# Picking one row of a group on VectorE instead of lowering the others in TensorE's sum

## The chip, the cores and the metric

One core of a Trainium2 chip runs the kernel; the other cores are idle. The metric is device time in microseconds, the median of three runs. Beside the timed runs there is one profiled execution, and all views below are of that one.

## The reference

The kernel computes one message-passing layer of a graph network. `x` has 12500 nodes of 32 features, `src` and `dst` name 400000 edges sorted by `dst`, and every edge has 32 attributes of its own.

```python
h = jnp.maximum(_layernorm(x, axis=-1), 0.0)
e_feat = jnp.concatenate([h[src], h[dst], edge_attr], axis=-1)   # 400000 x 96
v = jax.nn.relu(e_feat @ W1 + b1) @ W2 + b2                      # 96 -> 64 -> 32
x_cand = jax.ops.segment_max(v, dst, num_segments=12500)
out = x + jnp.maximum(x_cand, h)
```

Note that `h` is never negative, because of the relu after the normalisation.

## The kernel before

The edges are cut into four stripes (`NS`) that lie side by side on the partitions, 32 partitions each. A stripe is walked in 196 chunks of 512 edges (`NCH`, `C`), so a chunk holds 2048 edges. The main loop takes two chunks per turn (98 turns); `a` and `b` are the two chunks of the next turn, which are prepared while the current ones, `c` and `c+1`, are finished.

The rows `h[src]` of a chunk come to SBUF as 16 sets of 128 rows, in two ways:

- 12 sets are gathered from DRAM by indirect DMAs that GpSimd (POOL) issues, one per set (`gather`, L148: 2345 of them in all). They go into a ring of 24 buffers of three sets each, so POOL can run up to 72 sets ahead. Nothing else stands on POOL's queue during the loop.
- 4 sets (`MM`) are picked by TensorE from a copy of `h` that stays in SBUF (`hs`), split in a high and a low part of type fp32r. This is `tile(c, m)`, 780 times in all. The 12544 nodes are 128 partitions x 7 groups (`A1`) x 14 places (`A0`). `one_hots` builds, for each of the 7 groups, a 128x512 matrix `hot[:, k]` that has a one where the partition and the group are those of the edge's source: one VectorE tensor_scalar per group (L340) that compares the chunk's keys `kb` with a column of `key_p`. Fourteen matmuls (7 groups x 2 parts, L356) with moving operands of 448 columns sum up, in one PSUM bank `po`, all 14 nodes of the wanted group for each edge. To leave the right one of the 14, a fifteenth matmul (L353, bf16) comes first: `its`, a one-hot of the place (L342), times `others`, a constant with -1e30 at all other places. VectorE then takes the maximum over the 14 (L359), straight from PSUM.

`to_features` turns three gathered sets (L400) or the four picked ones (L403) into feature-major form `ht` by 32x32 transposes on VectorE. The rest of a turn: `into_ph` (L444) sums the three 64-wide products of an edge chunk in four PSUM banks `ph` (attributes by `edges_into`, the destination windows by `windows_into`, sources last); ScalarE applies the relu (`hid`, L491); the second product goes to two banks (L506); VectorE runs a maximum scan along the edges (L513); `leave_1` transposes the scan and adds the bias (`so`, L420, L422); `lasts` (L410) marks the last edge of each node; `leave_2` picks these rows (L430), ScalarE copies them (`wo`, L434), and SyncE (SP) writes them out. `window_hots` (L386, L387) builds the one-hots of the destination windows on ScalarE by a square and a relu. ScalarE's queue also issues the loads of `kb`, `db` and `pb`.

The order on PE, VectorE, ScalarE and SP is the order in which the code is written; no scheduler moves anything. The PSUM banks matter: `tile` and the second product share two buffers named `pv` in rotation. So a matmul group into `pv` waits until the group two before it has been read. [...]

A turn of the loop, in the order of writing (TensorE and VectorE parts):

```python
tile(a, 0); to_features(a, 0); into_ph(ht of c, c+1)      # then hid and window_hots on ScalarE
one_hots(b, range(3)); tile(a, 1); to_features(a, 1)
one_hots(b, range(3, A1)); lasts(c); tile(a, 2); to_features(a, 2)
edges_into(a); second product into pv, pv                 # L506
windows_into(a); leave(); scan, scan                      # L513
tile(a, 3); to_features(a, 3..J); leave_1(c); lasts(c + 1)
tile(b, 0); one_hots(a + 2, range(4)); leave_2(c); tile(b, 1); leave_1(c + 1)
one_hots(a + 2, range(4, A1)); tile(b, 2); tile(b, 3)     # each with its to_features
```

Ahead of the loop the layer normalisation, `hs`, the penalties and the checks are made, and the tiles of chunks 0 and 1 run by themselves.

Of the kernel before, what the change touches and what calls it, by code (L numbers as in the profile page):

```python
# [23 lines left out]
P = 128  # L24
N = 12500
E = 400000
D = 32
# [21 lines left out]
GP = 3  # L49
ROUND = 12582912.0  # L50
LOW = 1e30
ZERO = 784
WEIGHTS = 6 * HID + D + P + 1
EPS = 1e-5
# [2 lines left out]
def ap(t, offset, dims):  # L57
    return bass.AP(tensor=t.tensor, offset=t.offset + offset, ap=dims)
# [3 lines left out]
def gnn_kernel(ctx, tc, x, src, src_mm, src_t, dst, dst_next, dst_ext, lo, lo_c, hi, edge_attr, weights, w1, w2, b2, out):  # L62
# [26 lines left out]
    q_d = dram.tile([NP, HID], F32, name="q_d")  # L89
    pen_d = dram.tile([EP], BF16, name="pen_d")  # L90
    top_d = [dram.tile([NP, D], F32, name=f"top_d{k}") for k in range(2)]
    key_d = dram.tile([2, len(MMC) * MM * P], F16, name="key_d")
    acc_d = dram.tile([NP, D], F32, name="acc_d")
    v_d = dram.tile([P, D], F32, name="v_d")

# [21 lines left out]
    place = const.tile([P, 1], F32, name="place")  # L117
    nc.gpsimd.iota(place, pattern=[[0, 1]], base=0, channel_multiplier=1,
                   allow_small_or_imprecise_dtypes=True)
    key_p = const.tile([P, A1], F32, name="key_p")  # L120
    nc.gpsimd.iota(key_p, pattern=[[1, A1]], base=0, channel_multiplier=A1,
                   allow_small_or_imprecise_dtypes=True)
    hs = const.tile([P, 2, A1, D, A0], F32R, name="hs")
    others = const.tile([P, D, A0], BF16, name="others")


    wt = const.tile([P, WEIGHTS], F32, name="wt")
# [26 lines left out]
    with tc.tile_pool(name="nodes", bufs=1) as pool, tc.tile_pool(name="nodes_ps", bufs=2, space=PSUM) as ps:  # L154
# [10 lines left out]
        iota_a = pool.tile([P, D, A0], F32, name="iota_a")  # L165
        nc.gpsimd.iota(iota_a, pattern=[[0, D], [1, A0]], base=0, channel_multiplier=0,
                       allow_small_or_imprecise_dtypes=True)
# [15 lines left out]
        with tc.manual_schedule(engines={DVE, SP}):  # L183
# [35 lines left out]
            key16 = pool.tile([P, 2, len(MMC) * MM], F16, name="key16")  # L219
            nc.vector.tensor_copy(key16[:, 0], key)  # L220
            nc.vector.scalar_tensor_tensor(key16[:, 1], key, -float(A0), sp, op0=ALU.mult, op1=ALU.add)
            nc.sync.dma_start(key_d.rearrange("k (p e) -> p k e", p=P), key16)
# [84 lines left out]
    with tc.tile_pool(name="edges", bufs=3) as pool, tc.tile_pool(name="edges_ps", bufs=1, space=PSUM) as ps, \  # L307
# [3 lines left out]
        ofs = {}  # L311
        keys = {}
        hots = {}
        bases = {}
        iota_ps = ps.tile([P, C], F32, name="iota_ps")[:, :W]
        nc.vector.tensor_copy(iota_ps, iota_w)
        mm_rows = {}
        gh = {}
        hts = {}

        def load_keys(c):

            if c in MMC:
                n = min(2, MMC.stop - c)
                kb = pool.tile([P, 2, 2, MM * P], F16, name="kb", bufs=2)
                nc.scalar.dma_start(kb[:, :, :n], ap(key_d, (c - MMC.start) * MM * P,
                                                     [[0, P], [len(MMC) * MM * P, 2], [1, n * MM * P]]))
                for k in range(n):
                    keys[c + k] = kb[:, :, k]

        def one_hots(c, groups):

            if c not in MMC:
                return
            if c not in hots:
                hots[c] = (pool.tile([P, A1, MM * P], F32R, name="hot", bufs=2),
                           pool.tile([P, MM * P], BF16, name="its", bufs=2))
            hot, its = hots[c]
            for k in groups:
                nc.vector.tensor_scalar(hot[:, k], keys[c][:, 0], key_p[:, k:k + 1], None, op0=ALU.is_equal)  # L340
            if A1 - 1 in groups:
                nc.vector.tensor_scalar(its, keys.pop(c)[:, 1], place, None, op0=ALU.is_equal)  # L342

        def tile(c, m):

            if c not in MMC:
                return
            if m == 0:
                mm_rows[c] = pool.tile([P, MM, D], F32, name="gm", bufs=6)
            hot, its = hots[c]  # L350
            e = slice(m * P, (m + 1) * P)
            po = ps.tile([P, C], F32, name="pv", bufs=2)[:, :D * A0]
            nc.tensor.matmul(po, its[:, e], others.rearrange("p f a -> p (f a)"), start=True, stop=False)  # L353
            for k in range(A1):
                for part in range(2):
                    nc.tensor.matmul(po, hot[:, k, e], hs[:, part, k].rearrange("p f a -> p (f a)"),  # L356
                                     start=False, stop=(k == A1 - 1 and part == 1))
            rows = mm_rows[c][:, m, :]
            nc.vector.tensor_reduce(rows, po.rearrange("p (f a) -> p f a", a=A0), axis=AX.X, op=ALU.max)  # L359

        def load(c):
            if c % LOAD == 0:
# [26 lines left out]
        def to_features(c, part):  # L389

            if c >= NCH:
                return
            if c not in hts:
                hts[c] = pool.tile([P, K, D], F32, name="ht", bufs=4)
            ht = hts[c]
            n = min(K - MM * (c in MMC), (SE - c * C) // D)
            if part < J:
                r = slice(part * SOME, min((part + 1) * SOME, n))
                if r.start < n:
                    nc.vector.transpose(ht[:, r].rearrange("p k e -> p (k e)"),  # L400
                                        gh[c][part][:, :r.stop - r.start].rearrange("p k f -> p (k f)"))
# [74 lines left out]
        for c in range(0, NCH, 2):  # L476
# [33 lines left out]
            for x in range(2):  # L510
# [2 lines left out]
                nc.vector.tensor_tensor_scan(sm, loaded.pop(c + x)[2], pv[x], before, op0=ALU.add, op1=ALU.max)  # L513
# [178 lines left out]
```

## Time and profile before

| what | value |
|---|---|
| time, median of 3 runs | 3158.97 us (3158.54 to 3159.71) |
| profiled execution | 3161.57 us, its span 3159.8 us |
| granted TensorE clock | 0.983 |
| busy share of PE, DVE, ACT, POOL | 96%, 58%, 18%, 74% |
| matmuls of `tile` (L356, L353) | 10920 and 780 |
| gathers (L148) | 2345, the first at 31.1 us, the last at 3059.8 us |

A busy share is the union of the instructions' durations over the span. TensorE's instructions overlap each other, so what one of them costs is read from the distance between starts in the timeline, not from its duration. For VectorE and ScalarE the next instruction begins slightly before the last one's end when it doesn't depend on it. For POOL a gather has a duration and a constant pause behind it.

### The profile page before, as it was taken

What the parts mean: (1) busy time and instruction counts of PE and PEld (TensorE: products, weight loads), DVE (VectorE), ACT (ScalarE), POOL (GpSimd) and SP (SyncE); (2) the same over time, 40 slices, a digit from 0 to 9 for tenths busy, and PEclk for the clock granted to TensorE, in tenths of its full rate; (3) what the DMA queues carried; (4) which work ended last, traced back from release to release, by engine and by line L of the source; (5) the groups of instructions that cost most, each with busy time, mean ns of one, the idle gap of its engine ahead of it and who ended that gap; (6) DMA issues with size and microseconds to landing.
All of it is one profiled execution on the core that took longest, in us unless ns stands there. A gap on an engine that the chain in (4) does not pass through costs nothing. (4 is left out here: it accounts for less than half of the span.)

```text
span 3159.8 us, 59504 instructions
## 1 busy us (share of the span) xinstructions
PE 3038.9 (96%) x21969; PEld 2382.0 (75%) x21969; DVE 1822.4 (58%) x3999; ACT 562.8 (18%) x1007; POOL 2331.2 (74%) x2377
## 2 busy tenths in 40 slices
PE   2799999999999999999999999999999999999995
PEld 1578787777778777777778777777778777777873
DVE  6455555555555555555555555555555555555554
ACT  2121212112121212112121211112121211212121
POOL 7777777777777777777777777777777777777751
PEclk7899999999999999999999999999999999999997
DMA  6323332332333233233323332332333233233321
GB/s 246 109 64 74 90 73 63 90 80 68 72 89 76 64 84 83 71 69 89 78 64 77 88 72 63 90 83 64 73 89 76 64 87 85 66 72 88 78 57 63
DMA packets 203030, 255.38 MB, mean 81 GB/s; under 512 B 116062, under 2 KB 154862, under 8 KB 189551
## 3 DMA queue, kind: packets, MB, share of 16 engines
q10 hardware_dynamic: 42364, 138.10, 14.0%
q1 hardware_dynamic: 85330, 74.88, 10.1%
q0 software_dynamic: 75040, 38.57, 8.8%
q8 instruction: 173, 2.83, 0.4%
q14 instruction: 123, 1.00, 0.1%
HBM read 237.24 MB, written 14.05 MB: 80 GB/s over the span
## 5 line engine op out<-in xcount | busy, mean ns | idle before, releaser
L148 POOL DMA_INDIRECT gh<-h_d,src_i x2345 | 2301.2, 981 | 731.3 <-issue 567.8
L356 PE MATMUL pv<-hs,hot 128*128 128x448 f32 x10920 | 2435.0, 376 | 0.0
L356 PEld LDWEIGHTS pv<-hs,hot 128*128 128x128 f32 x10920 | 2058.5, 189 | 150.2 <-issue 0.3
L359 DVE TENSOR_REDUCE gm<-pv 128x32 f32<-128x448 f32 x780 | 486.3, 623 | 1149.9 <-PE pv L356 1147.7
L340 DVE TENSOR_SCALAR hot<-kb,key_p 128x512 fp32r<-128x512 f16 x1365 | 584.0, 487 | 6.1 <-DMA kb<-key_d 6.1
L491 ACT ACTIVATE hid<-ph,wt 128x512 f32<-128x512 f32 x392 | 237.2, 688 | 1325.7 <-PE ph L444 1312.2
L513 DVE TENSOR_TENSOR_SCAN sm<-pb,sm,pv 128x512 f32<-128x512 bf16 x195 | 249.6, 1280 | 133.4 <-PE pv L506 122.8
L353 PE MATMUL pv<-others,its 128*128 128x448 bf16 x780 | 281.3, 361 | 17.3 <-DMA qw<-q_d 10.6
L434 ACT ACTIVATE wo<-tr 128x64 f32<-128x64 f32 x196 | 43.7, 223 | 1146.6 <-PE tr L430 1056.4
L400 DVE STREAM_TRANSPOSE ht<-gh 128x96 f32<-128x96 f32 x782 | 209.5, 268 | 0.0
L353 PEld LDWEIGHTS <-its 128*128 128x128 bf16 x780 | 74.9, 96 | 172.4 <-issue 151.8
L430 PEld LDWEIGHTS tr<-so,last 128*64 128x64 f32 x3136 | 108.0, 138 | 112.6 <-issue 107.0
L386 ACT ACTIVATE of<-db,below 128x512 f32<-128x512 int32 x196 | 141.4, 721 | 64.5 <-DMA db<-in_dst_ext 64.5
L387 ACT ACTIVATE of<-of,ones 128x512 f32<-128x512 f32 x196 | 142.3, 726 | 6.4
L430 PE MATMUL tr<-so,last 128*64 128x64 f32 x3136 | 135.2, 229 | 3.3 <-DVE so L422 3.3
L410 DVE TENSOR_TENSOR last<-iota_ps,at 128x512 f32<-128x512 f32 x196 | 132.8, 678 | 0.0
L422 DVE TENSOR_TENSOR so<-tr,wt 128x512 f32<-128x512 f32 x196 | 127.9, 653 | 3.0 <-PE tr L420 3.0
L420 PE MATMUL tr<-ident,sm 128*128 128x128 f32 x784 | 117.8, 272 | 1.5 <-DVE sm L513 0.8
L444 PE MATMUL ph<-ht,wt 32*64 32x512 f32 x1568 | 111.3, 617 | 0.0
L420 PEld LDWEIGHTS tr<-ident,sm 128*128 128x128 f32 x784 | 97.4, 141 | 16.7 <-ACT wo L434 2.0
L506 PE MATMUL pv<-hid,wt 64*32 64x512 f32 x1568 | 109.3, 605 | 0.7 <-ACT hid L491 0.7
L444 PE MATMUL ph<-ea,wt 32*64 32x512 f32 x1568 | 109.1, 613 | 0.0
(78 smaller groups left out, 478.4 us busy)
## 6 DMA issues: line engine op xcount, KB each, us to landing
ea<-in_edge_attr SPq DMA_DIRECT2D x49, 1024.0 KB
db<-in_dst_ext ACTq DMA_DIRECT2D x49, 1024.0 KB
kb<-key_d ACTq DMA_DIRECT2D x97, 512.0 KB
gh<-h_d,src_i POOLq DMA_INDIRECT x2345
pb<-pen_d ACTq DMA_DIRECT2D x49, 512.0 KB
qw<-q_d SPq DMA_DIRECT2D x784, 8.0 KB
top_d<-wo SPq DMA_DIRECT2D x784, 4.0 KB
top_d<-zero ACTq DMA_DIRECT2D x2, 1568.0 KB
```

The lines of the kernel that those rows point to most:

```text
L148: nc.gpsimd.indirect_dma_start(out=parts[-1][:, i, :], out_offset=None, in_=h_d[:, :], in_offset=bass.IndirectOffsetOnAxis(ap=src_i[:, c, ...
L340: nc.vector.tensor_scalar(hot[:, k], keys[c][:, 0], key_p[:, k:k + 1], None, op0=ALU.is_equal)
L353: nc.tensor.matmul(po, its[:, e], others.rearrange("p f a -> p (f a)"), start=True, stop=False)
L356: nc.tensor.matmul(po, hot[:, k, e], hs[:, part, k].rearrange("p f a -> p (f a)"), start=False, stop=(k == A1 - 1 and part == 1))
L359: nc.vector.tensor_reduce(rows, po.rearrange("p (f a) -> p f a", a=A0), axis=AX.X, op=ALU.max)
L387: nc.scalar.activation(of, of, AF.Relu, bias=ones, scale=-1.0)
L400: nc.vector.transpose(ht[:, r].rearrange("p k e -> p (k e)"), gh[c][part][:, :r.stop - r.start].rearrange("p k f -> p (k f)"))
L420: nc.tensor.transpose(px[:, j, :], sm[:, j * P:(j + 1) * P], ident)
L430: nc.tensor.matmul(pw[g * 2 * W:(g + 1) * 2 * W], last[:, j, 2 * g:2 * g + 2].rearrange("p s w -> p (s w)"), so[:, j, g * 2 * D:(g + 1) * ...
L444: nc.tensor.matmul(ph[s][x * HID:(x + 1) * HID], w[g], e[g], start=start, stop=stop)
L491: nc.scalar.activation(hid[s], ph[s], AF.Relu, bias=b1c)
L513: nc.vector.tensor_tensor_scan(sm, loaded.pop(c + x)[2], pv[x], before, op0=ALU.add, op1=ALU.max)
```

## The change

The fifteenth matmul goes, with `its`, `others` and the second half of the keys in DRAM. In its place VectorE multiplies the PSUM bank with a one-hot of the place (`mask_of`: 128 x 4 x 14 per chunk, made from `place_k`, which is computed once ahead of the loop), writes 448 products per partition to SBUF (`one`), and takes the maximum of these (the products of the other places are zero, and `h` isn't negative). The one-hots of groups 0 to 4 become two VectorE tensor_tensors per chunk, of two and of three groups, whose second operand is `key_p` copied to the constants' PSUM bank; those of groups 5 and 6 (`BY_ACT`) go to ScalarE, a square and a relu each. `one_hots_act(b)` stands behind `window_hots` in a turn, `one_hots_act(a + 2)` behind `tile(a, 3)`.

```diff
+BY_ACT = range(A1 - 2, A1)
...
-    key_d = dram.tile([2, len(MMC) * MM * P], F16, name="key_d")
+    key_d = dram.tile([len(MMC) * MM * P], F16, name="key_d")
...
+    key_n = const.tile([P, A1], F32, name="key_n")
+    nc.gpsimd.iota(key_n, pattern=[[-1, A1]], base=0, channel_multiplier=-A1,
+                   allow_small_or_imprecise_dtypes=True)
...
-            nc.vector.scalar_tensor_tensor(key16[:, 1], key, -float(A0), sp, op0=ALU.mult, op1=ALU.add)
...
-            nc.vector.tensor_scalar(others, iota_a, place, -LOW, op0=ALU.not_equal, op1=ALU.mult)
+            group(pk, se)
+            nc.vector.scalar_tensor_tensor(pk, pk, -float(A0), se, op0=ALU.mult, op1=ALU.add)
...
-        iota_ps = ps.tile([P, C], F32, name="iota_ps")[:, :W]
+        consts = ps.tile([P, C], F32, name="consts")
+        iota_ps, key_ps = consts[:, :W], consts[:, W:W + A1]
         nc.vector.tensor_copy(iota_ps, iota_w)
+        nc.vector.tensor_copy(key_ps, key_p)
...
-                kb = pool.tile([P, 2, 2, MM * P], F16, name="kb", bufs=2)
-                nc.scalar.dma_start(kb[:, :, :n], ap(key_d, (c - MMC.start) * MM * P,
-                                                     [[0, P], [len(MMC) * MM * P, 2], [1, n * MM * P]]))
+                kb = pool.tile([P, 2, MM * P], F16, name="kb", bufs=2)
+                nc.scalar.dma_start(kb[:, :n], ap(key_d, (c - MMC.start) * MM * P,
+                                                  [[0, P], [MM * P, n], [1, MM * P]]))
                 for k in range(n):
-                    keys[c + k] = kb[:, :, k]
-
-        def one_hots(c, groups):
+                    keys[c + k] = kb[:, k]
+
+        def hot_of(c):
+            if c not in hots:
+                hots[c] = pool.tile([P, A1, MM * P], F32R, name="hot", bufs=2)
+            return hots[c]
+
+        def one_hots(c, start, stop):
             if c not in MMC:
                 return
-            if c not in hots:
-                hots[c] = (pool.tile([P, A1, MM * P], F32R, name="hot", bufs=2),
-                           pool.tile([P, MM * P], BF16, name="its", bufs=2))
-            hot, its = hots[c]
-            for k in groups:
-                nc.vector.tensor_scalar(hot[:, k], keys[c][:, 0], key_p[:, k:k + 1], None, op0=ALU.is_equal)
-            if A1 - 1 in groups:
-                nc.vector.tensor_scalar(its, keys.pop(c)[:, 1], place, None, op0=ALU.is_equal)
+            n = stop - start
+            nc.vector.tensor_tensor(hot_of(c)[:, start:stop], keys[c][:, None, :].to_broadcast([P, n, MM * P]),
+                                    key_ps[:, start:stop, None].to_broadcast([P, n, MM * P]), op=ALU.is_equal)
+
+        def one_hots_act(c):
+
+            if c not in MMC:
+                return
+            for k in BY_ACT:
+                away = pool.tile([P, MM * P], F32, name="away", bufs=2)
+                nc.scalar.activation(away, keys[c], AF.Square, bias=key_n[:, k:k + 1])
+                nc.scalar.activation(hot_of(c)[:, k], away, AF.Relu, bias=ones, scale=-1.0)
+
+        def mask_of(c):
+            if c in MMC:
+                masks[c] = pool.tile([P, MM, A0], F32, name="mask", bufs=2)
+                nc.vector.tensor_tensor(
+                    masks[c], iota_ps[:, None, :A0].to_broadcast([P, MM, A0]),
+                    place_k[:, (c - MMC.start) * MM:(c - MMC.start + 1) * MM, None].to_broadcast([P, MM, A0]),
+                    op=ALU.is_equal)
         def tile(c, m):
...
                 return
             if m == 0:
                 mm_rows[c] = pool.tile([P, MM, D], F32, name="gm", bufs=6)
-            hot, its = hots[c]
+            hot = hots[c]
             e = slice(m * P, (m + 1) * P)
             po = ps.tile([P, C], F32, name="pv", bufs=2)[:, :D * A0]
-            nc.tensor.matmul(po, its[:, e], others.rearrange("p f a -> p (f a)"), start=True, stop=False)
             for k in range(A1):
                 for part in range(2):
                     nc.tensor.matmul(po, hot[:, k, e], hs[:, part, k].rearrange("p f a -> p (f a)"),
-                                     start=False, stop=(k == A1 - 1 and part == 1))
-            rows = mm_rows[c][:, m, :]
-            nc.vector.tensor_reduce(rows, po.rearrange("p (f a) -> p f a", a=A0), axis=AX.X, op=ALU.max)
+                                     start=(k == 0 and part == 0), stop=(k == A1 - 1 and part == 1))
+            of_group = po.rearrange("p (f a) -> p f a", a=A0)
+            one = pool.tile([P, D, A0], F32, name="one", bufs=2)
+            nc.vector.tensor_tensor(one, of_group, masks[c][:, m, None, :].to_broadcast([P, D, A0]), op=ALU.mult)
+            nc.vector.tensor_reduce(mm_rows[c][:, m, :], one, axis=AX.X, op=ALU.max)
         def load(c):
             if c % LOAD == 0:
...
         for c in range(2):
             gh[c] = gather(c)
         for c in range(2):
-            one_hots(c, range(A1))
+            one_hots(c, 0, BY_ACT.start)
+            one_hots_act(c)
+            mask_of(c)
             for m in range(MM):
                 tile(c, m)
                 to_features(c, m)
             to_features(c, J)
-        one_hots(2, range(A1))
+        one_hots(2, 0, BY_ACT.start)
+        one_hots_act(2)
+        mask_of(2)
         ph = edges_into(0)
         windows_into(0, ph)
         sm = None
...
                 nc.scalar.activation(hid[s], ph[s], AF.Relu, bias=b1c)
             for k in range(a, min(a + 2, NCH)):
                 window_hots(k)
-            one_hots(b, range(3))
+            one_hots_act(b)
+            one_hots(b, 0, 2)
             tile(a, 1)
             to_features(a, 1)
-            one_hots(b, range(3, A1))
+            one_hots(b, 2, BY_ACT.start)
+            mask_of(b)
             last = [lasts(c)]
             tile(a, 2)
             to_features(a, 2)
...
                 nc.vector.tensor_tensor_scan(sm, loaded.pop(c + x)[2], pv[x], before, op0=ALU.add, op1=ALU.max)
                 sms.append(sm)
             tile(a, 3)
+            one_hots_act(a + 2)
             to_features(a, 3)
             to_features(a, J)
             so = leave_1(c, sms[0])
             last.append(lasts(c + 1))
             tile(b, 0)
             to_features(b, 0)
-            one_hots(a + 2, range(4))
+            one_hots(a + 2, 0, 2)
             leave_2(c, so, last[0])
             tile(b, 1)
             to_features(b, 1)
             so = leave_1(c + 1, sms[1])
-            one_hots(a + 2, range(4, A1))
+            one_hots(a + 2, 2, BY_ACT.start)
+            mask_of(a + 2)
             tile(b, 2)
             to_features(b, 2)
             tile(b, 3)
```

More of the change, by code (lines that the diff above doesn't have):

```diff
@@ L115, in gnn_kernel @@
                        allow_small_or_imprecise_dtypes=True)
-    place = const.tile([P, 1], F32, name="place")
-    nc.gpsimd.iota(place, pattern=[[0, 1]], base=0, channel_multiplier=1,
-                   allow_small_or_imprecise_dtypes=True)
     key_p = const.tile([P, A1], F32, name="key_p")
@@ L122, in gnn_kernel @@
                    allow_small_or_imprecise_dtypes=True)
+    key_n = const.tile([P, A1], F32, name="key_n")
+    nc.gpsimd.iota(key_n, pattern=[[-1, A1]], base=0, channel_multiplier=-A1,
+                   allow_small_or_imprecise_dtypes=True)
     hs = const.tile([P, 2, A1, D, A0], F32R, name="hs")
-    others = const.tile([P, D, A0], BF16, name="others")
+    place_k = const.tile([P, len(MMC) * MM], F32, name="place_k")
     wt = const.tile([P, WEIGHTS], F32, name="wt")
@@ L164, in gnn_kernel @@
         half = pool.tile([P, pieces[GP].stop - pieces[GP].start, D // 2], F32, name="half")
-        iota_a = pool.tile([P, D, A0], F32, name="iota_a")
-        nc.gpsimd.iota(iota_a, pattern=[[0, D], [1, A0]], base=0, channel_multiplier=0,
-                       allow_small_or_imprecise_dtypes=True)
         lo_w = pool.tile([P, NCH], I32, name="lo_w")
@@ L218, in gnn_kernel @@
             group(key, sp)
-            key16 = pool.tile([P, 2, len(MMC) * MM], F16, name="key16")
-            nc.vector.tensor_copy(key16[:, 0], key)
-            nc.vector.scalar_tensor_tensor(key16[:, 1], key, -float(A0), sp, op0=ALU.mult, op1=ALU.add)
-            nc.sync.dma_start(key_d.rearrange("k (p e) -> p k e", p=P), key16)
-            nc.vector.tensor_scalar(others, iota_a, place, -LOW, op0=ALU.not_equal, op1=ALU.mult)
+            key16 = pool.tile([P, len(MMC) * MM], F16, name="key16")
+            nc.vector.tensor_copy(key16, key)
+            nc.sync.dma_start(key_d.rearrange("(p e) -> p e", p=P), key16)
+            se = src_i[:, MMC.start:MMC.stop, K - MM:]
+            pk = place_k.rearrange("p (c m) -> p c m", m=MM)
+            group(pk, se)
+            nc.vector.scalar_tensor_tensor(pk, pk, -float(A0), se, op0=ALU.mult, op1=ALU.add)
             nc.vector.tensor_tensor(below, below, lo_w, op=ALU.subtract)
@@ L313, in gnn_kernel @@
         hots = {}
+        masks = {}
         bases = {}
-        iota_ps = ps.tile([P, C], F32, name="iota_ps")[:, :W]
+        consts = ps.tile([P, C], F32, name="consts")
+        iota_ps, key_ps = consts[:, :W], consts[:, W:W + A1]
         nc.vector.tensor_copy(iota_ps, iota_w)
+        nc.vector.tensor_copy(key_ps, key_p)
         mm_rows = {}
```

## The prediction

> **What bounds the kernel now.** First the page's busy shares, to see which engines are candidates.
>
> ```profile
> PE 3038.9 (96%) x21969; PEld 2382.0 (75%) x21969; DVE 1822.4 (58%) x3999; ACT 562.8 (18%) x1007; POOL 2331.2 (74%) x2377
> ```
>
> PE leads, but POOL's 74% hides something: its 2345 gathers are each followed by a pause. So next the timeline of one turn, engine by engine (start, duration, engine, line). TensorE:
>
> ```profile
> 1500.92 1.09 PE L506 MATMUL pv<-hid,wt 64*32 64x512 f32 x16
> ...
> 1527.57 0.36 PE L353 MATMUL pv<-others,its 128*128 128x448 bf16 x1
> 1527.61 3.20 PE L356 MATMUL pv<-hs,hot 128*128 128x448 f32 x14
> 1530.73 1.11 PE L444 MATMUL ph<-ea,wt 32*64 32x512 f32 x16
> 1531.78 0.66 PE L506 MATMUL pv<-hid,wt 64*32 64x512 f32 x8
> ```
>
> A turn is 1531.78 - 1500.92 = 30.86 us, and no row of it shows idle time: TensorE never waits. 98 turns make up 3024 of 3160 us. VectorE, between `tile(a,1)` and the second product of the same turn:
>
> ```profile
> 1527.77 0.62 DVE L359 TENSOR_REDUCE gm<-pv 128x32 f32<-128x448 f32 x1 [2.04 <-PE pv L356]
> 1528.31 0.27 DVE L400 STREAM_TRANSPOSE ht<-gh 128x96 f32<-128x96 f32 x1
> 1528.50 1.63 DVE L340 TENSOR_SCALAR hot<-kb,key_p 128x512 fp32r<-128x512 f16 x4
> 1530.05 0.35 DVE L342 TENSOR_SCALAR its<-kb,place 128x512 bf16<-128x512 f16 x1
> 1530.31 0.69 DVE L410 TENSOR_TENSOR last<-iota_ps,at 128x512 f32<-128x512 f32 x1
> 1530.91 0.61 DVE L359 TENSOR_REDUCE gm<-pv 128x32 f32<-128x448 f32 x1
> ```
>
> The last row has no idle time before it: here VectorE is late. It frees the second `pv` bank at 1531.52, and TensorE wants that bank at 1531.78. The slack is 0.26 us, the smallest of the turn. POOL in the same stretch:
>
> ```profile
> 1526.85 0.94 POOL L148 DMA_INDIRECT gh<-h_d,src_i  x1 [0.30 <-issue]
> 1528.09 0.97 POOL L148 DMA_INDIRECT gh<-h_d,src_i  x1 [0.30 <-DMA gh<-h_d,src_i]
> 1529.37 1.18 POOL L148 DMA_INDIRECT gh<-h_d,src_i  x1 [0.30 <-issue]
> 1530.85 0.95 POOL L148 DMA_INDIRECT gh<-h_d,src_i  x1 [0.30 <-issue]
> ```
>
> A gather takes 0.944 us (the median of its tile's view; the mean is 981 ns) and 0.30 us of pause, so 1.248 us from start to start, and 24 make 29.95 us a turn. From the first at 31.1 us to the last at 3059.8 us the mean is 3028.7 / 2344 = 1.292 us, or 31.0 us a turn: POOL is as slow as TensorE and lives on the lead it has at the start (the 48th gather starts near 93 us, its rows are wanted near 160; at the end the last at 3059.8, wanted at 3112.5). So two engines lie within 1%, and the gain on one is capped by the other.
>
> The rows of which the costs are made:
>
> ```profile
> L148 POOL DMA_INDIRECT gh<-h_d,src_i x2345 | 2301.2, 981 | 731.3 <-issue 567.8 <-DMA gh<-h_d,src_i 104.6 <-DVE ht L400 17.8
> L340 DVE TENSOR_SCALAR hot<-kb,key_p 128x512 fp32r<-128x512 f16 x1365 | 584.0, 487 | 6.1 <-DMA kb<-key_d 6.1
> L353 PE MATMUL pv<-others,its 128*128 128x448 bf16 x780 | 281.3, 361 | 17.3 <-DMA qw<-q_d 10.6 <-DVE its L342 6.3 <-DVE sm L513 0.3
> L386 ACT ACTIVATE of<-db,below 128x512 f32<-128x512 int32 x196 | 141.4, 721 | 64.5 <-DMA db<-in_dst_ext 64.5
> L410 DVE TENSOR_TENSOR last<-iota_ps,at 128x512 f32<-128x512 f32 x196 | 132.8, 678 | 0.0
> L422 DVE TENSOR_TENSOR so<-tr,wt 128x512 f32<-128x512 f32 x196 | 127.9, 653 | 3.0 <-PE tr L420 3.0
> L242 DVE TENSOR_TENSOR hs<-h,hs 128x896 fp32r<-128x896 f32 x3 | 4.9, 1711 | 0.0
> ```
>
> **The change part by part.** *The matmul that goes.* Its 281 us in the row are durations that overlap. Starts are what counts: two tiles in a row begin 3.01 us apart in the timeline (1517.33, 1520.34), others 3.08; the fp32r matmuls inside follow at 0.200 in the one and 0.207 in the other, so fourteen alone take 2.80 or 2.90, and the bf16 matmul is worth 0.18 to 0.21. The Trainium skill ("VectorE: DVE Perf Modes", section "The TRN2 errata") gives a matmul 6 + columns cycles at 2.4 GHz: 454 cycles, an estimate of 189 ns. By the row's duration the gain would be 281 us, by the rule 148, by the starts 780 x 0.195 = 152. I take 152: 1.56 us a turn.
>
> *Product and maximum.* The product reads PSUM and SBUF like L422 (653 ns at 512 elements): less 64 elements at 0.96 per ns, 586 ns. It frees the bank, as L359 did in 0.62. The maximum then reads SBUF; L174 does 896 elements in 1081, so 448 take about 615. A dependent instruction begins about 0.03 us after its forerunner (L291, L292 in the preparation), an independent one 0.08 before its end. A tile's share of VectorE grows from 0.54 to 0.62 + 0.54 = 1.16 us, 780 x 0.62 = 484 us in all. VectorE goes from 58% to about 70%, still no bound as a sum. What matters is where it is late.
>
> *One-hots.* Five groups of 512 in two tensor_tensors. Near rows are L410 and L290 (784 elements in 970 ns): elements at 0.96 per ns plus about 0.15. The pair takes 1.21 and 1.75 us, the mask of 56 elements 0.2, together 2.95 a chunk against 7 x 0.39 + 0.35 = 3.1 (L340 by its pitch in the burst of four). No gain.
>
> *The new wait.* From `tile(a,1)`'s end VectorE now runs: product and pause 0.62, maximum 0.54, transpose 0.19, one-hots of groups 2 to 4 1.67, mask 0.13, `lasts` 0.60, and the product of `tile(a,2)` 0.59: 4.34 us, and 0.05 until TensorE sees it. TensorE gets to the second product 1531.78 - 1527.77 = 4.01 us after that point, now 4.01 - 0.2 = 3.81. It waits 0.58 us; I take 0.6 per turn, 97 x 0.6 = 58 us. Behind this matmul stand `windows_into`, `leave` and `tile(a,3)`, so all of the turn slips by it; VectorE's scan, which waits for that product, slips as much. Elsewhere cover remains: `tile(b,2)`'s product comes 0.4 us late, but its bank is needed one tile later.
>
> *ScalarE.* Four more activations a chunk at about 0.72 (L386): 195 x 2.9 = 560 us, 18% to 36%. Those of `b` stand between `window_hots` and the copy `wo` of the last `leave`: from the first `hid` 2.4 + 2.9 + 2.9 = 8.2 us, while `wo` is wanted 9.9 us after it. Nothing waits. Those of `a+2` start after `tile(a,3)` and take 2.9 us, and the next `wo` comes 3.9 us after that point. Cost nothing; if an activation that writes fp32r took 1.1 us, the margins would be gone but little more. The `kb` loads on ScalarE's queue halve in size (512 to 256 KB), and no order on SP changes.
>
> *The beginning.* On ScalarE the one-hots of chunk 0 stand behind `window_hots`, which waits for `db` until 107.5 us (64.5 us of wait in its row). Four activations there and four here end near 112, some 2 us earlier if the halved `kb` load lets `db` land earlier. `tile(0,0)` ended at 100.8 and can't end before 111.5 now: 11 us, plus about 1 for chunk 1, whose one-hots VectorE makes behind it. 12 us (8 to 15). Nothing covers that, since POOL is ahead there. `place_k` adds 3 ops of 0.6 to 1 us, in VectorE's idle time ahead of the penalties (2.0 and 9.9 us).
>
> *POOL.* Its stretched gathers (1.18 above) lie, over the whole trace, beside L340 and L342, not beside L359, L422 or the scans alone. Their excess is 2345 x (981 - 944) ns = 87 us. The Trainium skill ("SBUF — State Buffer", section "SBUF: two separate sides") says that VectorE instructions in a 2-port mode, tensor_scalar among them, lock GpSimd out, and that one with at most one SBUF input outside these modes doesn't. In the new loop no such tensor_scalar is left; every tensor_tensor has one operand in PSUM. By the rule POOL's last gather moves to about 3061 - 87 = 2974; by the row alone, which can't tell the port from the mere load on VectorE, it stays at 3061. I take 2974. TensorE's turn of 30.86 - 1.56 + 0.6 = 29.9 is then the like of POOL's 29.95, and POOL keeps its lead of over 50 us.
>
> *The sum.* 3159.8 - 152 + 58 + 12 = 3078 span. The profiled run reads 1.8 us more than its span and 2.6 more than the median: 3077.
>
> **The rivals.** *POOL stays stretched.* If the port isn't the cause, or a maximum that reads SBUF takes its place, the last gather still ends at 3061, and about 47 us of tail follow (last transpose at 3112.5, end at 3159.8) with 2 to 4 for landing: 3112. For it: POOL has no wait on anybody now. Against it: the tail of stretched gathers goes with L340 and L342 alone.
>
> *The wait doesn't arise.* If VectorE's chain is 0.6 us shorter, TensorE alone would end at 3020, and POOL at 2974 + 50 = 3024 binds. Against it: the old chain had 0.26 us of slack, and 0.8 is added.
>
> *Slower: the three-group one-hot is slow.* The only tensor_tensor with fp32r output, L242, takes 1711 ns for 896 elements (958 for 448), 1.68 ns an element. The 1536 elements would then take 2.6 us instead of 1.67, the wait becomes 1.55 us or more, and the sum is 3159.8 - 152 + 12 + 97 x 1.6 = 3175. It decides from a wait of 140 / 97 = 1.44 us, a one-hot of about 2.5 us. Against it: L340 writes fp32r at under 0.95 ns an element, and L242 writes with a stride and reads two SBUF operands.
>
> *It doesn't do what it says.* If the fp32r weight load (189 ns) set the pace, the bf16 matmul might be free; the starts of 3.01 against 14 x 0.200 exclude that.
>
> **How the numbers follow.** The sum as worked out 0.70; POOL stretched 0.08; no wait 0.08; one-hot slow 0.08; others, as a second wait of 0.8 us a turn that I have not seen, 0.06, half of it without a difference and half slower. The likeliest case by itself spans 3045 to 3110: the wait from 0.3 to 0.9 us is 29 us to either side, the matmul 0.18 to 0.21 11 us, the beginning 4. The range of 3020 to 3122 takes in both POOL-bound cases and leaves out the slow one. Faster by over 0.2% (6 us, what a measurement can tell here) 0.86, within it 0.03, slower 0.11.
>
> **What would show it.** L353 gone, and tiles that follow each other 2.8 to 2.9 us apart. A turn of 29.9 us. In it, one wait of TensorE for VectorE, before the second product, of about 0.6. Gathers with a mean near 950 ns and the last near 2975 us. TensorE's first tile held up until about 111 us. The one-hot rows at 1.2 and 1.75 us. A turn over 30.8, one-hots over 2.5 us, or a mean gather still at 981 with transposes that wait for gathers would prove me wrong.

## The result: less than half of the gain that was forecast

The changed kernel takes 3128.04 us (median of four runs, 3126.44 to 3129.87) against 3159.34 for the kernel before, a ratio of 0.990 (0.9884 to 0.9915). The forecast was 3077, its range 3020 to 3122: the sign was right, and the gain is 31 us where 82 were expected. The profiled execution took 3126.44 us, its span is 3124.7 and its granted clock 0.98.

The busy shares on the page after, for the same engines as shown before:

```profile
PE 2988.9 (96%) x21189; PEld 2330.7 (75%) x21189; DVE 2256.1 (72%) x3804; ACT 1084.0 (35%) x1787; POOL 2244.5 (72%) x2376
```

TensorE still leads at 96%. VectorE rose from 58% to 72% and ScalarE from 18% to 35%, both near what was worked out (70% and 36%). The timeline of TensorE over one turn, from one second product (L506 before, L532 now) onward:

```profile
1522.87 1.11 PE L464 MATMUL ph<-ea,wt 32*64 32x512 f32 x16
1523.91 1.70 PE L532 MATMUL pv<-hid,wt 64*32 64x512 f32 x16
1525.54 1.11 PE L464 MATMUL ph<-of,qw 32*64 32x512 f32 x16
1526.58 0.69 PE L450 MATMUL tr<-so,last 128*64 128x64 f32 x16
1527.20 3.13 PE L374 MATMUL pv<-hs,hot 128*128 128x448 f32 x14
1530.16 0.60 PE L440 MATMUL tr<-ident,sm 128*128 128x128 f32 x4
```

The second product's sixteen matmuls now last 1.70 us in the row where they lasted 1.09: from start to the start of the next work 1.63 instead of 1.02 us. They are merged into one row, so the wait in their middle shows only in the length. VectorE ahead of it:

```profile
1520.11 0.62 DVE L378 TENSOR_TENSOR one<-pv,mask 128x448 f32<-128x448 f32 x1 [1.54 <-PE pv L374]
1520.77 0.62 DVE L379 TENSOR_REDUCE gm<-one 128x32 f32<-128x448 f32 x1
1521.31 0.27 DVE L420 STREAM_TRANSPOSE ht<-gh 128x96 f32<-128x96 f32 x1
1521.50 1.72 DVE L343 TENSOR_TENSOR hot<-kb,consts 128x1536 fp32r<-128x1536 f16 x1
1523.13 0.20 DVE L358 TENSOR_TENSOR mask<-consts,place_k 128x56 f32<-128x56 f32 x1
1523.26 0.68 DVE L430 TENSOR_TENSOR last<-consts,at 128x512 f32<-128x512 f32 x1
1523.86 0.61 DVE L378 TENSOR_TENSOR one<-pv,mask 128x448 f32<-128x448 f32 x1
```

This is the chain that the prediction wrote down, from the end of `tile(a,1)` at 1520.11 to the end of the next product at 1524.47: 4.36 us, forecast 4.34. The last product has no idle time before it, so VectorE is late and TensorE waits for the bank. So the wait came as forecast. What did not come is the rest of the gain. Three stretches of the trace add up to the difference of the spans:

| stretch | before | after | difference |
|---|---|---|---|
| start of the span to the first second product | 143.3 | 160.6 | +17.4 |
| 97 turns, second product to second product | 2974.3 | 2922.2 | -52.1 |
| last second product to the end | 42.2 | 41.8 | -0.4 |

The turn goes from 30.85 to 30.30 us (means of turns 20 to 80, from the starts of TensorE's matmuls). In it the second product takes 0.62 us more, which is the wait, and all the rest 1.17 less, where 1.56 had been expected. The gathers in the view of their tile:

```profile
L148 POOL DMA_INDIRECT gh<-h_d,src_i x2345: 938/944/2288, 26.9 to 3002.8; - x196
L420 DVE STREAM_TRANSPOSE ht<-gh x782: 203/269/271, 117.1 to 3078.0; 128x96 f32<-128x96 f32 x196
```

The last gather starts at 3002.8 us and its rows are transposed 75 us later; before, that lead was 53. POOL doesn't bind. Their mean duration is 946 ns (981 before), so the stretched ones are nearly gone.

### The profile page after: what moved, and what is told of

It is laid out like the page before. It is cut to its first block, busy times and chain, and to the rows that moved or that the text cites. A ratio compares the mean times of both kernels' runs of the same rounds, so it can differ in the third digit from the quotient of the medians.

```text
span 3124.7 us, 58725 instructions
## 1 busy us (share of the span) xinstructions
PE 2988.9 (96%) x21189; PEld 2330.7 (75%) x21189; DVE 2256.1 (72%) x3804; ACT 1084.0 (35%) x1787; POOL 2244.5 (72%) x2376
## 5 line engine op out<-in xcount | busy, mean ns | idle before, releaser
L148 POOL DMA_INDIRECT gh<-h_d,src_i x2345 | 2218.8, 946 | 761.0 <-issue 552.4
L374 PE MATMUL pv<-hs,hot 128*128 128x448 f32 x10920 | 2358.9, 371 | 34.2 <-ACT hot L353 16.5
L374 PEld LDWEIGHTS pv<-hs,hot 128*128 128x128 f32 x10920 | 2017.0, 188 | 292.9 <-issue 97.4
L378 DVE TENSOR_TENSOR one<-pv,mask 128x448 f32<-128x448 f32 x780 | 484.1, 621 | 741.2 <-PE pv L374 741.2
L343 DVE TENSOR_TENSOR hot<-kb,consts 128x1024 fp32r<-128x1024 f16 (+2 forms) x387 | 566.7, 1464 | 5.7 <-DMA kb<-key_d 5.7
L379 DVE TENSOR_REDUCE gm<-one 128x32 f32<-128x448 f32 x780 | 484.0, 620 | 26.9
L353 ACT ACTIVATE hot<-away,ones 128x512 fp32r<-128x512 f32 x390 | 282.3, 724 | 235.6 <-issue 226.0
L352 ACT ACTIVATE away<-kb,key_n 128x512 f32<-128x512 f16 x390 | 276.5, 709 | 2.8 <-DMA qw<-q_d 2.8
L420 DVE STREAM_TRANSPOSE ht<-gh 128x96 f32<-128x96 f32 x782 | 209.8, 268 | 0.0
L450 PEld LDWEIGHTS tr<-so,last 128*64 128x64 f32 x3136 | 107.9, 138 | 113.8 <-issue 77.9
L532 PE MATMUL pv<-hid,wt 64*32 64x512 f32 x1568 | 168.7, 606 | 0.7 <-ACT hid L515 0.7
L450 PE MATMUL tr<-so,last 128*64 128x64 f32 x3136 | 135.0, 229 | 3.9 <-DVE so L442 3.9
L430 DVE TENSOR_TENSOR last<-consts,at 128x512 f32<-128x512 f32 x196 | 132.1, 674 | 0.0
L532 PEld LDWEIGHTS pv<-hid,wt 64*32 64x32 f32 x1568 | 30.9, 105 | 129.1 <-DVE hot L343 77.1
L440 PE MATMUL tr<-ident,sm 128*128 128x128 f32 x784 | 117.8, 273 | 1.3 <-ACT wo L454 0.7
L464 PE MATMUL ph<-ht,wt 32*64 32x512 f32 x1568 | 111.1, 617 | 0.2 <-DVE ht L426 0.2
```

The source lines that it names most:

```text
L148: nc.gpsimd.indirect_dma_start(out=parts[-1][:, i, :], out_offset=None, in_=h_d[:, :], in_offset=bass.IndirectOffsetOnAxis(ap=src_i[:, c, ...
L343: nc.vector.tensor_tensor(hot_of(c)[:, start:stop], keys[c][:, None, :].to_broadcast([P, n, MM * P]), key_ps[:, start:stop, None].to_broad ...
L352: nc.scalar.activation(away, keys[c], AF.Square, bias=key_n[:, k:k + 1])
L353: nc.scalar.activation(hot_of(c)[:, k], away, AF.Relu, bias=ones, scale=-1.0)
L378: nc.vector.tensor_tensor(one, of_group, masks[c][:, m, None, :].to_broadcast([P, D, A0]), op=ALU.mult)
L379: nc.vector.tensor_reduce(mm_rows[c][:, m, :], one, axis=AX.X, op=ALU.max)
```

## The experiments

Two things called for tests: why TensorE gives back less than the starts of the tiles suggested, and what the parts of the change are worth one by one. Unless another number of runs is named, the times are medians of four runs, with ratios to the kernel before.

**The start.** The one-hots of chunks 0 to 2 ahead of the loop are all made on VectorE.

```diff
-            one_hots(c, 0, BY_ACT.start)
-            one_hots_act(c)
+            one_hots(c, 0, A1)
...
-        one_hots(2, 0, BY_ACT.start)
-        one_hots_act(2)
+        one_hots(2, 0, A1)
```

> The changed kernel with the one-hots of chunks 0, 1 and 2 all on VectorE (seven groups in one tensor_tensor, nothing of them on ScalarE); the loop is unchanged. Theory: the start costs 17.4 us because ScalarE's two groups stand behind window_hots, which waits for db. Then the first L532 comes at 143 to 146 us instead of 160.6, the turn stays at 30.30, and the time is 3128 - 16 = 3112. Rival: something else that needs db or qw holds the start, and less than 5 us come back: 3123 to 3128.

Measured: 3112.83 us, ratio 0.985 (0.983 to 0.987). The first second product starts at 148.0 us, a little later than expected, and the turn stays at 30.30. So two groups on ScalarE ahead of the loop cost 12.6 us at the first second product, and 15 by the medians. The other 4.8 of the 17.4 us stay. In this run TensorE stops for the masks of chunks 1 and 2 for 5.61 and 3.71 us, where it stopped at the same places for 4.10 and 2.20 before the change, which is 3.0 of the 4.8.

**The wait.** The first `lasts` of a turn goes from ahead of the second product to behind the scans.

```diff
             mask_of(b)
-            last = [lasts(c)]
             tile(a, 2)
...
                 sms.append(sm)
+            last = [lasts(c)]
             tile(a, 3)
```

> The changed kernel with the first lasts of a turn (0.60 us on VectorE) moved from ahead of the product of tile(a,2) to behind the two scans, where VectorE idles for 2.0 us. Theory: the 0.62 us wait of TensorE ahead of the second product is VectorE's chain alone. Then the wait falls to 0.0 to 0.1, the turn to 29.7, and the time by 97 x 0.6 = 58 to 3070. Rival 1: the wait moves on (to tile(a,3), leave_2 or the next turn) and the turn stays over 30.1: 3110 or more. Rival 2: POOL binds at 24 gathers x 1.25 = 30.0 a turn: TensorE shows waits for transposes late in the run, 3090 to 3100.

Measured: 3068.52 us, ratio 0.971 (0.969 to 0.973). TensorE's timeline:

```profile
1525.83 1.11 PE L464 MATMUL ph<-ea,wt 32*64 32x512 f32 x16
1526.88 1.12 PE L531 MATMUL pv<-hid,wt 64*32 64x512 f32 x16
1527.93 1.11 PE L464 MATMUL ph<-of,qw 32*64 32x512 f32 x16
```

The sixteen matmuls are back at 1.12 us. The turn falls to 29.69 us, 0.61 less, and the time by 59.5 us. So the wait goes whole and doesn't come up elsewhere, and its cause is VectorE's order.

**The removal alone.** The kernel before, without the bf16 matmul and its one-hot; it takes the maximum over the whole group instead of the edge's own node, so it leaves out the picking.

```diff
-            if A1 - 1 in groups:
-                nc.vector.tensor_scalar(its, keys.pop(c)[:, 1], place, None, op0=ALU.is_equal)
...
-            nc.tensor.matmul(po, its[:, e], others.rearrange("p f a -> p (f a)"), start=True, stop=False)
```

> The kernel before without the bf16 matmul and the one-hot of the place; it leaves out the choice among the 14, so the maximum runs over the whole group. Nothing else is changed: seven tensor_scalars, maximum from PSUM, no ScalarE part. If the matmul is worth 1.2 us a turn on TensorE (0.15 a tile) and nothing else binds: turn 29.65, time 3159 - 117 = 3042. If it is worth the 1.56 that the prediction took: 3007. If POOL, whose gathers stay stretched by the tensor_scalars (mean 965 to 980 ns), binds in the end: last gather near 3025 to 3061, waits of VectorE for gathers late in the run, and 3075 to 3112.

Measured: 3119.81 us, ratio 0.987 (0.985 to 0.989): 40 us gained, less than either free case. The gathers' view, and a line of the list of waits (us in total, times, longest):

```profile
L148 POOL DMA_INDIRECT gh<-h_d,src_i x2345: 938/944/1656, 30.2 to 3067.3; - x196
L398 DVE STREAM_TRANSPOSE ht<-gh x782: 200/268/284, 98.1 to 3071.8; 128x96 f32<-128x96 f32 x196
```

```profile
DVE ht L398 <- DMA gh<-h_d,src_i: 151.8, 103, 3.8
```

The last gather starts 4.5 us before the last transpose, and VectorE waits 103 times for rows that are still on their way. POOL, with a mean gather of 983 ns, is the bound here, as the third expectation said, though its range ended at 3112 us. For the price of the matmul the time of this run is only a bound. Its median turn, 29.63 us, doesn't wait for POOL and is near the 29.65 that were expected for 1.2 us a turn; its tiles take 23.56 us a turn, as in the change (23.59).

**The matmul put back, as zeros.** Three kernels add to the change a bf16 matmul of zeros at the head of each tile (it adds nothing to the sum): in all tiles; in the three that follow matmuls on a part of the array (L464 with 32 rows, L450 with 64 columns); and in the other five, which follow another tile or the 128x128 transposes of L440. Each ran once. The cut is of the second kernel.

```diff
+            extra = (c % 2, m) in ((0, 1), (0, 3), (1, 1))
+            if extra:
+                nc.tensor.matmul(po, nil_w, nil_m, start=True, stop=False)
...
-                                     start=(k == 0 and part == 0), stop=(k == A1 - 1 and part == 1))
+                                     start=(k == 0 and part == 0 and not extra), stop=(k == A1 - 1 and part == 1))
```

> The changed kernel with a bf16 matmul of zeros (128 rows, 448 columns, constant operands) put ahead of the fourteen of each tile; the sum is not altered. It measures what the removed matmul costs TensorE now. Theory (the fp32r weight load behind a matmul on a part of the array is not hidden, and the bf16 matmul hid it): the stretches of the eight tiles grow by 1.2 us a turn, and the first fp32r matmul of each run follows at the normal pitch; with the wait 0.2 shorter the turn is 31.3. Rival (a full slot of 0.2 each): 1.6, turn 31.7.

> The changed kernel with the bf16 matmul of zeros only in the three tiles of a turn that follow a matmul on a part of the array: tile(a,1) behind into_ph, tile(a,3) behind leave, tile(b,1) behind leave_2. Theory of the weight load: there the first fp32r pair now stands 0.309 us apart, and the bf16 matmul takes 0.2 but gives 0.1 back. Turn 30.30 + 0.3 = 30.6, the pair behind the bf16 matmul at 0.37 including its 0.2 of cover. Rival 1 (a full slot of 0.2 each): 30.9. Rival 2 (0.15 for every tile alike): 30.75.

> The changed kernel with the bf16 matmul of zeros only in the other five tiles of a turn, which follow fp32r tiles or the full-array transposes of leave_1. Theory of the weight load: 0.195 each, 0.97 on TensorE, less 0.2 because tile(a,2) is one of them and gives VectorE that much more time ahead of the second product: turn 30.30 + 0.77 = 31.07. Rival (0.15 for every tile alike): 0.75 - 0.2, turn 30.85.

Measured: 3245.53, 3171.39 and 3214.66 us; turns of 31.51, 30.73 and 31.23. The turns alone decide nothing: the first lies between the theory (31.3) and its rival (31.7), the second next to the rival of 0.15 us for every tile (30.75), the third above both its numbers. The fp32r matmuls also follow each other at 205.3 ns instead of 204.0, which is 0.13 to 0.14 us a turn by itself and for which the runs show no reason. The starts decide: from the start of the last instruction ahead of a tile to that of its second fp32r matmul, mean over turns 20 to 80, in ns (the zeros of the first two rows are from the kernel with three, those of the others from the one with five).

| ahead of the tile | before | change | with zeros |
|---|---|---|---|
| L450 (L430 before), part of the array | 559 | 461 | 562 |
| L464 (L444), part of the array | 929 | 827 | 922 |
| L440 (L420), 128x128 transposes | 505 | 315 | 507 |
| another tile | 606 | 409 | 615 |

A matmul at the head of a tile is worth 0.10 us in the first two rows and 0.19 to 0.21 in the others, much the same when it is taken away and when it is put back. Outside the second product and without the pitch, three zeros cost 0.31 us of a turn and five cost 1.01, so 0.10 and 0.20 each.

**Tensor_scalar again for groups 0 to 4.**

```diff
-            n = stop - start
-            nc.vector.tensor_tensor(hot_of(c)[:, start:stop], keys[c][:, None, :].to_broadcast([P, n, MM * P]),
-                                    key_ps[:, start:stop, None].to_broadcast([P, n, MM * P]), op=ALU.is_equal)
+            for k in range(start, stop):
+                nc.vector.tensor_scalar(hot_of(c)[:, k], keys[c], key_p[:, k:k + 1], None, op0=ALU.is_equal)
```

> The changed kernel with the one-hots of groups 0 to 4 made as before, one tensor_scalar per group with the key as a [128,1] scalar in SBUF, and not by tensor_tensors with an operand in PSUM. On VectorE this is quicker (3 x 0.39 against 1.67 us in the chain ahead of the second product), so TensorE's wait falls from 0.62 to about 0.15. Theory of the port: the gathers are stretched again (mean 970 to 981 ns), the last one moves from 3003 to 3060 to 3090, VectorE waits for gathers late in the run, and the time is 3110 to 3140 in spite of the shorter wait. Rival (only the load on VectorE stretched them): mean 946 to 950, the time 3128 - 46 = 3082.

Measured: 3094.80 us, ratio 0.980 (0.979 to 0.982): between the two theories, and 33 us faster than the change. VectorE's timeline and the gathers:

```profile
1527.86 1.24 DVE L343 TENSOR_SCALAR hot<-kb,key_p 128x512 fp32r<-128x512 f16 x3
1529.02 0.20 DVE L357 TENSOR_TENSOR mask<-consts,place_k 128x56 f32<-128x56 f32 x1
1529.14 0.67 DVE L429 TENSOR_TENSOR last<-consts,at 128x512 f32<-128x512 f32 x1
1529.74 0.60 DVE L377 TENSOR_TENSOR one<-pv,mask 128x448 f32<-128x448 f32 x1
```

```profile
L148 POOL DMA_INDIRECT gh<-h_d,src_i x2345: 938/944/1712, 27.1 to 3040.8; - x196
L419 DVE STREAM_TRANSPOSE ht<-gh x782: 199/268/280, 120.5 to 3046.6; 128x96 f32<-128x96 f32 x196
```

Three tensor_scalars take 1.16 us to the start of the mask where the three-group tensor_tensor takes 1.63 (1521.50 to 1523.13 above). TensorE's wait falls from 0.62 to 0.18 us (means of turns 20 to 80). The stretched gathers return: a mean of 968 ns, the last at 3040.8, its transpose 5.8 us later. So the cause of the stretching was told rightly, but its price here is small: VectorE waits 28 us in all for gathers, 17 of them after 2700 us.

**All groups on VectorE.**

```diff
-BY_ACT = range(A1 - 2, A1)
+BY_ACT = range(A1, A1)
```

> The change with the one-hots of all seven groups made on VectorE, none on ScalarE. If the chain on VectorE ahead of the second product sets the turn, it grows by two tensor_tensors of 0.53 us, 1.07 us: TensorE's wait there goes from 0.62 to about 1.7 us and the turn from 30.30 to about 31.35, 97 turns 103 us more; the start comes back by about 15 us as no one-hot stands behind window_hots on ScalarE: about 3216 us, slower than before. If VectorE has room for them (it is busy 72% of the time), 3130 us or less.

The first try took 4301.81 us and the kernel before 4113.76 beside it, at a granted clock of 0.889 for both, so its times stand beside no other here. Once more:

> The one-hots of all seven groups made on VectorE, none on ScalarE, once more: the run before had a granted clock of 0.889 for both kernels. At 0.98, if the chain on VectorE ahead of the second product sets the turn, the wait there goes from 0.62 to about 1.7 us, the turn from 30.30 to about 31.35, the start comes back by about 15 us: about 3216 us. If VectorE has room for two groups more, 3130 us or less.

Measured: 3215.48 us (two runs, 3215.08 and 3215.88; before 3160.29), ratio 1.017 (1.015 to 1.020). VectorE's and TensorE's timelines:

```profile
1524.59 2.78 DVE L343 TENSOR_TENSOR hot<-kb,consts 128x2560 fp32r<-128x2560 f16 x1
1527.30 0.20 DVE L358 TENSOR_TENSOR mask<-consts,place_k 128x56 f32<-128x56 f32 x1
1527.42 0.67 DVE L430 TENSOR_TENSOR last<-consts,at 128x512 f32<-128x512 f32 x1
1528.02 0.61 DVE L378 TENSOR_TENSOR one<-pv,mask 128x448 f32<-128x448 f32 x1
```

```profile
1527.00 1.04 PE L532 MATMUL pv<-hid,wt 64*32 64x512 f32 x2
1528.68 1.09 PE L532 MATMUL pv<-hid,wt 64*32 64x512 f32 x14 [0.64 <-DVE one L378]
```

Five groups in one instruction take 2.71 us to the mask's start, 1.08 more than three. Now the wait is long enough to part the row: fourteen of the sixteen matmuls begin 1.68 us after the first two. The turn is 31.37 us and the first second product is at 147.1. The two groups on ScalarE are thus worth 87 us in this order: about 103 through the chain ahead of the second product (97 turns of 1.07), less the 13.5 that the start gets back.

**Both mends together:** the start on VectorE and the later `lasts`, the edits of the first two experiments.

> The changed kernel with both edits of the first two runs: the one-hots of chunks 0 to 2 on VectorE, and the first lasts of a turn behind the scans. If the two costs add: 3128 - 15 - 60 = 3053. Rival: POOL binds now, since its last gather came at 3010 in both runs and the transposes of the last turn would be wanted at 3005: 3055 to 3065, with waits of VectorE for gathers in the last turns.

Measured: 3056.92 us (five runs), ratio 0.968 (0.967 to 0.970), the fastest of all: 71 us below the change and 102 below the kernel before. The turn is 29.70, the first second product at 148.8. The last gather stands at 3003.9 and its transpose 6.2 us later, so POOL is now nearly the bound too. The time lies in the range that was given for POOL as the bound, but VectorE waits only 5 us in all for gathers.

## Why the prediction was wrong

**The matmul that goes** is the step that failed: "1.56 us a turn" was 1.17, and 152 us were about 114. The prediction took the distance between the starts of two tiles in a row and compared it with fourteen matmuls "inside". That is the right price for a tile that follows a tile (197 ns, last row of the table), and holds behind the 128x128 transposes (190). But it was applied to all 780, and three of eight tiles per turn follow matmuls on a part of the array. There the gain was 98 and 102 ns. The sum is 2 x 0.19 + 3 x 0.197 + 3 x 0.10 = 1.27, less 0.09 for fp32r matmuls that follow each other at 204.0 ns instead of 203.1: 1.18, where 1.17 was measured. Over 97 turns this is 38 us of the 47 by which the sum of spans (3078 against 3124.7) was off; the beginning is 5, the wait 2, and 2 are not attributed.

What the trace shows there is the first weight load. Behind `leave`'s L450, in the changed kernel (two narrow cuts of the timeline):

```profile
1527.20 0.19 PEld L374 LDWEIGHTS pv<-hs,hot 128*128 128x128 f32 x1
1527.20 0.47 PE L374 MATMUL pv<-hs,hot 128*128 128x448 f32 x1
...
1527.20 0.67 PE L374 MATMUL pv<-hs,hot 128*128 128x448 f32 x2
1527.31 0.40 PEld L374 LDWEIGHTS pv<-hs,hot 128*128 128x128 f32 x2
...
1530.49 0.19 PEld L374 LDWEIGHTS pv<-hs,hot 128*128 128x128 f32 x1
1530.52 0.45 PE L374 MATMUL pv<-hs,hot 128*128 128x448 f32 x1
```

PEld's first row is the load of the run's first matmul: it begins with its matmul, not ahead of it. That first matmul lasts 0.47 us where others last 0.36, and the second, which ends at 1527.87, starts 0.31 behind the first instead of 0.20. The loads after it run beside the matmul before. The last two rows are of the next tile, behind the transposes of L440: there the load begins at 1530.49 together with the last transpose. Over turns 20 to 80 the first load of a tile begins 2 to 3 ns after the start of the last instruction ahead in the five places that gained 0.19 or more; in the other three it begins 150 ns (L450) or 516 (L464) after that start, and 2 ns ahead of its own matmul. In the kernel before, behind the same `leave`, stood:

```profile
1503.59 0.10 PEld L353 LDWEIGHTS <-its 128*128 128x128 bf16 x1
1503.60 0.20 PEld L356 LDWEIGHTS pv<-hs,hot 128*128 128x128 f32 x1
```

There the uncovered load was the bf16 one, 0.10 us, and the fp32r load of 0.20 ran beside the bf16 matmul. So the matmul that went had been half paid back by hiding a load twice as long as its own. The Trainium skill ("TensorE: Matmul & The Clock Gate", section "Step-by-step: what each phase is for") says that a load is pulled ahead of matmuls under way when its row groups don't conflict or it goes to the background weights. With every load pulled ahead all eight would have gained 0.2; which of the page's conditions fails behind L464 and L450 no run here shows. A wait it is not, as the first load of `tile(b, 1)`, behind L450, has none in the trace. That the worth depends on what stands ahead is shown by the runs with zeros; that it is the load, and not another cost of changing the array's use, is read from these starts and was not tried apart. The prediction's fourth rival ("it doesn't do what it says") had this mechanism in hand and dropped it for all tiles on the evidence of one kind.

**The new wait** was right: 0.6 forecast, 0.62 measured, its chain 4.36 us for 4.34, and 59.5 us gone when `lasts` leaves the chain. The product took 621 ns (586 forecast), the maximum 620 (615).

**The beginning** was undersized: 12 us forecast (8 to 15), and +17.4 measured at the first second product, although the first tiles are shorter too. ScalarE's timeline:

```profile
108.37 0.72 ACT L407 ACTIVATE of<-of,ones 128x512 f32<-128x512 f32 x1
111.52 0.33 ACTq L328 DMA_DIRECT2D kb<-key_d  x1
111.89 0.72 ACT L352 ACTIVATE away<-kb,key_n 128x512 f32<-128x512 f16 x1 [2.80 <-DMA qw<-q_d]
112.65 0.72 ACT L353 ACTIVATE hot<-away,ones 128x512 fp32r<-128x512 f32 x1
```

The four activations of `window_hots` end at 109.1, near the forecast, but the next load of `kb` stands on the same queue ahead of the one-hots, and they begin 2.8 us later. The prediction counted the activations in front, not the queue's DMA issue between them. TensorE:

```profile
113.42 1.12 PE L374 MATMUL pv<-hs,hot 128*128 128x448 f32 x2 [16.29 <-ACT hot L353]
114.79 10.38 PE L374 MATMUL pv<-hs,hot 128*128 128x448 f32 x44 [0.25 <-ACT hot L353]
```

The three stretches behind it in which matmuls ran at half the granted clock, in the view by windows (the clock stands behind POOL's count):

```profile
113.40:117.40 4.00, 3.73 (x9) 2.88 (x10) 1.43 (x3) 3.90 (x7) 3.09 (x4) 0.50 0.39 79
129.70:134.40 4.70, 4.68 (x13) 4.23 (x14) 0.00 (x0) 0.00 (x0) 3.48 (x5) 0.50 0.56 89
148.10:151.50 3.40, 3.40 (x9) 3.05 (x10) 0.00 (x0) 0.00 (x0) 2.49 (x4) 0.50 0.35 109
```

TensorE stands still for 16.29 us in the middle of `tile(0,0)`. Some tiles behind it are slower as well: `tile(2,0)` takes 4.65 us against 3.13 before. Each of the three stretches stands behind a stop of TensorE, of 16.29, 4.54 and 2.65 us. They are 12.1 us in all; before the change 6.8 us of matmuls ran so from the first tile on (96 to 100 us and 114.2 to 117), so an estimate of what the clock added is half the difference, 2.7 us. The prediction had no term for it. With all one-hots on VectorE the first second product comes 12.6 us earlier.

**ScalarE in the loop** cost nothing, as forecast (724 ns for an activation that writes fp32r, 35% busy). **The one-hots** took 1182 and 1726 ns (1.21 and 1.75 forecast), so the slower rival fell. "No gain" from them was right for their sum and wrong for the piece that matters: the three groups that stand in the chain cost 0.47 us more than three tensor_scalars.

**POOL** was right in cause and in effect, not in the place of its last gather. The excess of the mean gather over 944 ns fell from 87.6 us in all to 5.1, as worked out. The Trainium skill ("SBUF — State Buffer", section "SBUF: two separate sides") says that a tensor_scalar can enter a mode that locks GpSimd out of a shared port, and that an instruction with at most one SBUF input outside such modes doesn't contend with it. The tensor_tensors of the change have one operand in PSUM. The run with tensor_scalars (55 us of excess) agrees. The mere load on VectorE isn't the cause, since VectorE is busier in the change (72%) than before (58%); that it is the port, no run here shows apart. But the time of the pauses above 0.304 us, their usual length, rose from 15.8 to 45.6 us, so the last gather starts at 3002.8 and not at 2974. The kernel with tensor_scalars and the new product had 33.1, the one with tensor_scalars and without the product 20.5. In six pauses of the changed kernel, 6 us in all, POOL waits for a buffer of its ring; for the rest why is open. It cost nothing here; with the start and the wait mended it is what stands next.

## What to carry to other kernels

Price a TensorE instruction at each place where it occurs, by the starts around it: where it heads a run behind matmuls on a part of the array, it may be hiding the next weight load, and taking it away gives only the difference. When work is added to an engine, add up the chain ahead of the one wait with the least slack; a single 0.6 us instruction moved out of it was worth twice what the whole change was. An instruction that spares another engine (the tensor_tensor here) pays only if that engine is the bound at its new pace, and a slower form in the critical chain can cost more than it spares.

## What the runs showed of the hardware that was not expected

- An fp32r load of 128x128 weights takes 0.19 to 0.20 us and a bf16 one 0.10. Behind matmuls on a part of the array (32 rows, or 64 columns) the first load of a run of fp32r matmuls began only with its own matmul, and the first two matmuls stood 309 ns apart, against 204 inside a run. Behind 128x128 transposes the load began with the last transpose, and inside a run with the matmul before; no such loss showed there.
- A mean gather takes 983 ns beside seven tensor_scalars a chunk, 968 beside five and 946 beside none; the median is 944 in each.
- At the beginning the granted clock was 0.50 for 3.4 to 4.7 us of matmuls behind stops of TensorE of 2.65 to 16.29 us.
- A DMA issue on ScalarE's queue held up the activations behind it for 2.8 us until it could be issued.
- At a mean granted clock of 0.889 the kernel before took 4114 us, 30% more for a clock lower by 10%. The trace of the kernel with all groups on VectorE (turns of 42.7 us there, 31.4 at 0.982) shows that the clock isn't where this time goes. Of the 11.3 us a turn, 4.1 stand at the second product, 3.0 at the attributes' L464 and 2.8 at `tile(b, 2)` and `tile(b, 3)`, where TensorE stops; `tile(b, 0)` takes 3.03 us in both runs. What it stops for was not followed.
